# Graph network kernel, one core: the keys of the third pair of logits parted 330 and 330 instead of 512 and 148

## The chip, the cores and the metric

The kernel runs on one NeuronCore of one Trainium2 chip. The metric is device time in microseconds (us), start to end of one execution; a timed run is one such execution, and the number compared is the median of several. The names of the engines follow the profile: PE is TensorE (matmuls; PEld is its weight load), DVE is VectorE, ACT is ScalarE, POOL is GpSimd, SP is SyncE, which here only issues transfers.

## The reference

Two graph layers over N = 2708 nodes with D = 256 features, float32. Layer 0 adds one graph convolution to x and normalises. Layer 1 takes two steps. In each, an attention matrix over all nodes is made from queries and keys of width 64, thinned to the largest probabilities of each row that together hold 0.9, and multiplied on the features; beside it, the features are spread by the normalised adjacency matrix R. Cut to what matters:

```
q = X @ W1.T @ W2.T ;  k = X @ W3.T
logits = q @ k.T                       # 2708 x 2708, contraction over 64
probs  = softmax(logits)               # then the top-p entries of each row alone are kept
A      = kept / sum(kept)
R      = (S + I) / rowsum(S + I)
for n in 0, 1:
    A  = top_p_attention(Xa)
    Xf = R @ Xf
    Xa = A @ Xa
    Z  = Z + Xf @ U1[n].T + Xa @ U2[n].T
out = layernorm(X + Z), added to X and normalised again
```

## The kernel before, in words

Rows of the node set are worked on in 22 blocks of 128 (the last has 20). The features lie transposed in the on-chip memory where they feed projections, and block by block where they are multiplied by attention weights.

**Queries and keys.** `qk_project` (L420 on) makes queries and keys of a range of columns with one stationary operand of 128 columns, 64 of which give the key and 64 the query: two matmuls (L426) into one "misc" buffer of PSUM, and then three copies on ACT (L428, L429, L430): the query goes to both halves of the partitions, the key to one half only. Keys are kept in pairs of chunks: the first chunk of a pair lies on one half of the partitions, the second on the other, so that a pair of logits matmuls can use the two halves of the array. Chunks are 512 wide: 0, 512, 1024, 1536, 2048, 2560, and the last holds 148. In step 0 `qk_project` is called for one chunk at a time, in the loop over the adjacency matrix; in step 1 for one block of 128 columns, from `project` in `step1_out`, where it is followed by one more projection into a "misc" buffer (L699), whose sum with x is taken by DVE (L702). There are two "misc" buffers.

**Logits.** `logits(s, t, i)` makes pair i (0, 1, 2) of block t: two matmuls with a contraction of 64, one per half of the partitions, into the two banks of the one "lg" buffer (L507). Each float32 matmul is two records in the profile. ACT empties the buffer over both banks in one instruction: as a copy (L514) in the first attention step, as an exponential (L844, and L848 for the first pair) in the second. The third pair has 512 and 148 columns.

**Stages.** After the adjacency loop (28 to 286 us) comes a prologue: the logits of blocks 0, 1 and 2, three pairs each, with projections by U1 (L651) between them, then DVE's extraction of the largest candidates (L570, L577, L579), ACT's exponentials (L613) and DVE's mask (L635). Then the first attention step: 22 iterations of the block loop, 17.5 us each (343 to 718 us). In each, a block's weights are transposed on PE in six groups (L527), copied by ACT (L530) and multiplied on the features (L564); the logits of the block three ahead stand at groups 0, 1 and 2, and the projections of the block before (L692, L426, L699) at groups 2 and 3. POOL gathers the non-zero rows of the adjacency matrix meanwhile (L367). From 718 to 748 us the projections for the second step (L672) run, with the third pairs of the second step's blocks 0, 1 and 2 between them.

The second step (748 to the end) has a period of 23 to 24 us per block. PE transposes and multiplies the weights of one block (L527, L564), makes the logits of a later one (third pair at group 3 of six) and runs `r_units`, the products by R: 22 blocks for each of the two steps, of eight matmuls each (L749), the rows for which POOL gathers by indirect transfers, seven per block (L719), into two buffers. ACT and DVE search the threshold meanwhile (L966, L969 on ACT; L1023, L1030, L1039, L1083 and L1088 on DVE). POOL also does two elementwise instructions per finished block (L1207, L1208), for which ACT normalises first (L1192). The last gathered block of the first product by R has to be stored before the first gather of the second may start.

The order of the instructions on each engine is written out by hand: the lists and generators in the code fix it, and no scheduler changes it. PE and POOL, like the others, work in that order.

Of the kernel before, what the change touches and what calls it, by code (L numbers as in the profile page):

```python
# [9 lines left out]
FP = mybir.dt.float32  # L10
# [10 lines left out]
P = 128  # L21
CH = 512
# [20 lines left out]

def chunks(N):
    return [(a, min(N, a + CH)) for a in range(0, N, CH)]


class Common:
# [4 lines left out]
def gnn_two_layer_kernel(ctx: ExitStack, tc: tile.TileContext, N, xT_d, x_d, adj_d, w0_d, b0_d,  # L53
# [30 lines left out]
    assert SEG * (NS - 1) + 8 <= N <= SEG * NS == SEG2 * NS2 and N >= SEG2 * (NS2 - 1) + 8  # L84
    assert NB == 3 * KS + 1 and CW == P and CAP % 8 == 0 and N < NB * P
    CHS = chunks(N)
    KH = NB // 2

# [36 lines left out]
    with fast:  # L125
        fast_path(fast, tc, c, flags, fint, xT_d, x_d, w0_d, b0_d, w1_d, w2_d, w3_d, u1_d, u2_d, g_d, b_d)
# [22 lines left out]
def fast_path(ctx, tc, c, flags, fint, xT_d, x_d, w0_d, b0_d, w1_d, w2_d, w3_d, u1_d, u2_d, g_d, b_d):  # L149
    nc = tc.nc  # L150
    N, D, DA, NB, DC, KH, CHS, rows = c.N, c.D, c.DA, c.NB, c.DC, c.KH, c.CHS, c.rows
# [5 lines left out]
    big = ctx.enter_context(tc.tile_pool(name="big", bufs=1))  # L157
# [5 lines left out]
    def ps_lg():  # L163
        return ps.tile([P, 2, CH], FP, tag="lg", name="lg", bufs=1)
# [10 lines left out]
    def ps_misc():  # L175
        return ps.tile([P, CH], FP, tag="misc", name="misc")
# [91 lines left out]
    at = NB * (NB - 1)  # L268
# [119 lines left out]
    for t in range(NB):  # L388
        p = rows(t)
        py = ps_misc()  # L390
        for j in range(DC):
            nc.tensor.matmul(py[:p, :D], lhsT=xT[:, j, t * P:t * P + p], rhs=w0[:, DC + j, :],  # L392
                             start=j == 0, stop=j == DC - 1)
# [8 lines left out]


    q = big.tile([P, N], FP, tag="Q", name="q")
    keys = [big.tile([P, (len(CHS) + 1) // 2, CH], FP, tag=f"K{s}", name=f"k{s}") for s in range(2)]


    wqkq = small.tile([P, DC, 3, DA], FP, tag="wqkq", name="wqkq", bufs=1)
# [10 lines left out]
    def qk_project(s, a, b, src):  # L419


        n, i, h = b - a, a // CH // 2, a // CH % 2
        po = ps_misc()
        for j in range(DC):
            w = wqkq[:, j, 1 - h:3 - h].rearrange("p h a -> p (h a)")
            nc.tensor.matmul(po[:, :n], lhsT=w, rhs=src(j), start=j == 0, stop=j == DC - 1)  # L426
        own, other = (slice(DA * g, DA * g + DA) for g in (h, 1 - h))
        nc.scalar.copy(q[other, a:b], po[other, :n])  # L428
        nc.scalar.copy(q[own, a:b], po[other, :n])  # L429
        nc.scalar.copy(keys[s][own, i, a % CH:a % CH + n], po[own, :n])  # L430

    x1T = big.tile([P, DC, N], FP, tag="B", name="x1T")

# [7 lines left out]
    def x1_qk(i):  # L441
        a, b = CHS[i]
        qk_project(0, a, b, lambda j: x1T[:, j, a:b])
# [3 lines left out]
    for m in range(NB):  # L447
        p = rows(m)
# [12 lines left out]
        for j in range(DC):  # L461
            nc.tensor.matmul(acc[:p, :D], lhsT=xT[:, j, m * P:m * P + p], rhs=w0[:, j, :],  # L462
                             start=False, stop=j == DC - 1)
# [6 lines left out]
        h = work.tile([P, D], FP, tag="mid", name="h")  # L470
# [12 lines left out]
        if m >= ML:  # L483
            i = m - ML
# [9 lines left out]
    x1_transpose(NB - 1)  # L494
    x1_qk(len(CHS) - 1)

    NL = (len(CHS) + 1) // 2

    def logits(s, t, i):


        p = rows(t)
        lg = ps_lg()
        cs = CHS[2 * i:2 * i + 2]
        for h, (a, b) in enumerate(cs):
            o = slice(DA * h, DA * h + DA)
            nc.tensor.matmul(lg[:p, h, :b - a], lhsT=q[o, t * P:t * P + p], rhs=keys[s][o, i, :b - a],  # L507
                             start=True, stop=True)
        a, b = cs[0][0], cs[-1][1]
        return lg.rearrange("p h n -> p (h n)")[:p, :b - a], a, b  # L510

    def logits1(t, i):
        lg, a, b = logits(0, t, i)
        nc.scalar.copy(es[t % 4][:rows(t), a:b], lg)  # L514
# [165 lines left out]
    def step1_out(t, acc, ra):  # L680

        p = rows(t)
        xaT = xaT_all[:, :, t * P:t * P + p]
        xa = work.tile([P, D], FP, tag="in", name="xa", bufs=3)

        def scale():
            nc.scalar.activation(xa[:p], acc[:p, :D], AF.Copy, scale=ra[:p])

        def turn_out():
            tr = ps_tr()  # L690
            for j in range(DC):
                nc.tensor.transpose(tr[:, j, :p], xa[:p, j * P:(j + 1) * P], ident[:p, :p])  # L692
            nc.scalar.copy(xaT[:, :, :p], tr[:, :DC, :p])

        def project():
            qk_project(1, t * P, t * P + p, lambda j: xaT[:, j, :p])
            pz = ps_misc()
            for j in range(DC):
                nc.tensor.matmul(pz[:p, :D], lhsT=xaT[:, j, :p], rhs=c.u2[:, j, 0, :],  # L699
                                 start=j == 0, stop=j == DC - 1)  # L700
            za = work.tile([P, D], FP, tag="mid", name="za")
            nc.vector.tensor_add(za[:p], pz[:p, :D], x1[:p, t, :])  # L702
            nc.sync.dma_start(out=za_d[t * P:t * P + p, :], in_=za[:p])

        return scale, turn_out, project
# [144 lines left out]
    def begin_search(b):  # L850

        nc.vector.tensor_reduce(b.z, b.all[:b.p, :NL], AX.X, ALU.add)
        yield
# [13 lines left out]
    def begin1(t, n):  # L867
        nonlocal n_u
        for i in range(NL):
            logits1(t, i)  # L870
# [21 lines left out]
    at = {(m // 2, 3 * (m % 2) + 1): m for m in range(4)}  # L892
# [4 lines left out]
    for t in range(NB):  # L897
        acc = ps_acc(t)
        part = exps1(t + 2) if t + 2 < NB else None
        b = None  # L900
        if t >= NB - 3:
            b = blocks[t - (NB - 3)] = Block(t - (NB - 3))
        ra_next = finish1(t + 1) if t + 1 < NB else None
        for g in range(NG):
            turn(t, g, x1, acc, es[t % 4])
            if ends and 1 <= g <= 3:
                ends[g - 1]()
            if g < NL and t + 3 < NB:
                logits1(t + 3, g)
            if b and g in (0, 2):  # L910
                lg = logits(1, b.t, g // 2)
                if g == 0:
                    shift(b, lg[0])
# [33 lines left out]
    for t in range(3):  # L947
        exps2(blocks[t], 2, *logits(1, t, 2))
        ya_pair()
# [5 lines left out]
    w = tile1[:, NW:]  # L955
# [315 lines left out]
    lg = logits(1, 3, 0)  # L1271
# [3 lines left out]
    for per in range(NB + 2):  # L1275
# [11 lines left out]
        for g in range(NG):  # L1287
            n = n_r * (g + 1) // NG - n_r * g // NG
# [13 lines left out]
            if b_exp and g == 3:  # L1302
                lg = logits(1, b_exp.t, 2)
            if g == NG - 1 and 3 < per + 3 < NB:
                lg = logits(1, per + 3, 0)
            if g:
                r_units(n)
            if b_exp and g == 1:
                lg = logits(1, b_exp.t, 1)
# [8 lines left out]
            if g == 0:  # L1318
                final_slot(0)
                if t_mul:  # L1320
                    t = t_mul - 1
# [6 lines left out]
    t = EDGE  # L1328
# [24 lines left out]
    n = len(new) + len(finals)  # L1353
# [381 lines left out]
```

## Time and profile before

| | us |
|---|---|
| three timed runs, median | 1295.33 |
| their lowest and highest | 1294.3, 1296.72 |
| the profiled execution | 1291.2 |
| its span, first to last instruction | 1289.4 |

The page of the profile is of that one execution. Its first part gives, for each engine, the time in which it was busy, that as a share of the span, and the number of instructions. A group names line, engine, operation, what is written from what (out<-in), the shape, the count, busy time, mean ns of one, and the idle time of the engine just before, with what ended it. A wait names what the engine was released by. In the timeline, equal neighbours are merged into one row: start, length, and xcount. In the chain, each piece is followed back to what released it. The mean granted clock of PE was 0.986 of full speed. The 528 records of the logits matmuls (L507) had a median of 589 ns each.

### The profile page before, as it was taken

How to read it: one execution, taken by the hardware profiler on the slowest of the kernel's cores; microseconds unless marked ns; L12 is line 12 of the kernel's file. 1: busy time of each engine (PE TensorE's matmuls, PEld its weight loads, DVE VectorE, ACT ScalarE, POOL GpSimd, SP SyncE). 2: the span in 40 equal slices, each digit the busy share in tenths (PEclk: the TensorE clock that was granted, in tenths of full speed). 3: DMA queues.
4: the chain of work that ended last, by engine and by line, in shares of the span. 5: the costliest groups of instructions: out<-in, count | busy, mean ns of one | idle time of the engine just before them, and what ended most of it. 6: DMA issues, size and time to landing. Idle time of an engine off the chain costs nothing.

```text
span 1289.4 us, 18741 instructions
## 1 busy us (share of the span) xinstructions
PE 1226.3 (95%) x5764; PEld 888.1 (69%) x5764; DVE 973.9 (76%) x3252; ACT 735.5 (57%) x1337; POOL 635.9 (49%) x594
## 2 busy tenths in 40 slices
PE   8999999979899999999999987999999999999885
PEld 6878777843477777777777555777766777767664
DVE  2445545884999997977872179889888999999886
ACT  2000110125456656556655488887888989989822
POOL 1000000003475452577756058878874878888860
PEclk9999999999999999999999988999999999999998
DMA  7455445423322210122224244565563545565451
GB/s 196 152 193 170 143 149 168 149 90 107 121 82 83 72 57 28 43 88 91 93 85 100 63 149 150 178 189 177 180 154 118 179 155 154 165 195 158 145 139 39
DMA packets 101703, 165.99 MB, mean 129 GB/s; under 512 B 17362, under 2 KB 74070, under 8 KB 101594
## 3 DMA queue, kind: packets, MB, share of 16 engines
q1 hardware_dynamic: 75308, 108.65, 26.0%
q0 software_dynamic: 20544, 51.17, 14.3%
q10 hardware_dynamic: 5742, 4.89, 1.3%
q8 instruction: 48, 0.79, 0.2%
q14 instruction: 61, 0.50, 0.1%
HBM read 130.74 MB, written 33.90 MB: 128 GB/s over the span
## 4 chain that ended last, share of the span: by engine, by line
PE 79%; DVE 8%; ACT 7%; DMA 3%; POOL 2%; issue 2%; ACTq 0%; POOLq 0%; DVEq 0%
PE acc L564 27%; PE acc L257 16%; PE lg L507 9%; PE misc L749 8%; PE tr L527 7%; PE acc L651 2%; DMA yg<-v_d,ix 2%; PE acc L462 2%; PE misc L392 2%; PE misc L426 2%; PE acc L672 2%; ACT e L966 2%; PE misc L699 1%; DVE e L1088 1%; ACT e L844 1%
## 5 line engine op out<-in xcount | busy, mean ns | idle before, releaser
L530 ACT COPY wT<-tr 128x512 f32<-128x512 f32 (+2 forms) x258 | 132.1, 519 | 208.7 <-PE tr L527 208.7
L564 PE MATMUL acc<-x,wT 128*128 128x256 f32 (+1 forms) x924 | 230.5, 388 | 0.0
L564 PE MATMUL acc<-ya,wT 128*128 128x256 f32 (+1 forms) x924 | 227.1, 385 | 0.0
L719 POOL DMA_INDIRECT yg<-v_d,ix x154 | 194.8, 1265 | 59.6 <-issue 22.6
L564 PEld LDWEIGHTS acc<-x,wT 128*128 128x128 f32 (+1 forms) x924 | 165.2, 189 | 71.0 <-issue 37.4
L719 POOL DMA_INDIRECT yg<-yf_d,ix x154 | 188.2, 1222 | 48.3 <-issue 22.5
L257 PE MATMUL acc<-y,adj_t 128*128 128x257 f32 (+1 forms) x924 | 208.4, 381 | 0.0
L564 PEld LDWEIGHTS acc<-ya,wT 128*128 128x128 f32 (+1 forms) x924 | 170.2, 190 | 44.4 <-issue 24.0
L749 PE MATMUL misc<-yg,adj_t 128*128 128x256 f32 (+1 forms) x704 | 183.7, 394 | 14.9 <-DMA yg<-v_d,ix 5.9
L367 POOL DMA_INDIRECT adj_t<-in_adj,ix x154 | 171.3, 1112 | 52.0 <-issue 41.8
L257 PEld LDWEIGHTS acc<-y,adj_t 128*128 128x128 f32 (+1 forms) x924 | 171.8, 189 | 32.7 <-issue 8.9
L749 PEld LDWEIGHTS misc<-yg,adj_t 128*128 128x128 f32 (+1 forms) x704 | 123.6, 189 | 67.6 <-issue 23.4
L507 PE MATMUL lg<-k,q 64*128 64x512 f32 (+3 forms) x528 | 149.5, 594 | 13.7 <-ACT e L848 7.0
L527 PE MATMUL tr<-ident,e 128*128 128x128 f32 (+2 forms) x946 | 147.1, 274 | 3.1 <-DVE e L1088 2.0
L527 PEld LDWEIGHTS tr<-ident,e 128*128 128x128 f32 (+2 forms) x946 | 112.2, 138 | 44.8 <-issue 16.4
L334 POOL DMA_DIRECT2D part_d<-e x1 | 0.6, 573 | 285.6 <-DVE e L333 285.6
L439 ACT COPY x1T<-tr 128x256 f32<-128x256 f32 (+1 forms) x22 | 8.0, 364 | 186.6 <-PE tr L438 186.6
L966 ACT ACTIVATE e<-e,st 128x2708 f32<-128x2708 f32 (+1 forms) x43 | 113.5, 2639 | 0.1
L969 ACT ACTIVATE e<-e,st 128x2708 f32<-128x2708 f32 (+1 forms) x42 | 110.9, 2641 | 0.1
L570 DVE MAX8 cand<-e 128x8 f32<-128x170 f32 (+1 forms) x352 | 87.2, 318 | 26.7 <-ACT e L514 26.7
L1030 DVE MAX8 cand<-w 128x8 f32<-128x170 f32 (+1 forms) x352 | 94.2, 321 | 0.0
L1083 DVE MATCH_REPLACE8 w<-part,e 128x680 f32<-128x680 f32 (+1 forms) x88 | 74.3, 851 | 0.0
(238 smaller groups left out, 1696.4 us busy)
## 6 DMA issues: line engine op xcount, KB each, us to landing
adj_t<-in_adj SPq DMA_DIRECT2D x44, 704.0 KB
adj_t<-adjc_d SPq DMA_DIRECT2D x44, 448.0 KB
adjc_d<-adj_t SPq DMA_DIRECT2D x22, 256.0 KB
base<-za_d SPq DMA_DIRECT2D x40, 128.0 KB
adjc_d<-adj_t SPq DMA_DIRECT2D x22, 192.0 KB
xt<-in_x ACTq DMA_DIRECT2D x21, 128.0 KB
x_d<-x SPq DMA_DIRECT2D x21, 128.0 KB
x1b_d<-xb SPq DMA_DIRECT2D x21, 128.0 KB
```

The source lines that it names most:

```text
L257: nc.tensor.matmul(acc[:p, :n], lhsT=halves[k // KH][:kw, k % KH, :p], rhs=y[:kw, k, :n], start=k == 0, stop=stop and k == NB - 1)
L367: nc.gpsimd.indirect_dma_start(out=a[:CW, i, :], out_offset=None, in_=adj_rows, in_offset=bass.IndirectOffsetOnAxis(ap=ix[:CW, m, i:i + 1] ...
L507: nc.tensor.matmul(lg[:p, h, :b - a], lhsT=q[o, t * P:t * P + p], rhs=keys[s][o, i, :b - a], start=True, stop=True)
L527: nc.tensor.transpose(tr[:kw, k % 4, :p], e[:p, k * P:k * P + kw], ident[:p, :p])
L530: nc.scalar.copy(wT[:, :full, :p], tr[:, :full, :p])
L564: nc.tensor.matmul(acc[:p, :D], lhsT=wT[:kw, k % 4, :p], rhs=y[:kw, k, :], start=k == 0, stop=k == NB - 1)
L570: nc.vector.max(dst[:p, i * 8:(i + 1) * 8], src[:p, i * step:i * step + w])
L719: nc.gpsimd.indirect_dma_start(out=y[:CW, i, :], out_offset=None, in_=rows_d, in_offset=bass.IndirectOffsetOnAxis(ap=ix[:CW, m, i:i + 1], ...
L749: nc.tensor.matmul(acc[:p, :D], lhsT=a[:kw, k, :p], rhs=y[:kw, k, :], start=k == 0, stop=k == CC)
L966: nc.scalar.activation(scr[:b.p, :N], e, AF.Relu, bias=b.nz, scale=b.l[k], accum_out=b.relu)
L969: nc.scalar.activation(scr[:b.p, :N], e, AF.Sign, bias=b.nz, scale=b.l[k], accum_out=b.sign)
L1030: nc.vector.max(b.cand[:p, 8 * i:8 * i + 8], low[:p, SEG2 * i:SEG2 * (i + 1)])
```

## The change

The borders of the keys move. `key_parts` cuts N into ranges of 1024 columns and each range in the middle: 0, 512, 1024, 1536, 2048, 2378, 2708. The first four parts are as before; the third pair now has 330 and 330 columns. `logits` places the first half of a pair at the end of its bank (from column 182 of 512 for the third pair), so that the two halves still lie side by side across the border of the two banks, and ACT's instruction reads 660 columns as before. `qk_project` goes over the parts that a range of columns touches and does the whole of its work for each. In step 0 that divides the chunk of columns 2048 to 2560 in two (330 and 182); in step 1 it divides block 18, columns 2304 to 2432 (74 and 54). In the built program the first L699 matmul after block 18 waits for PE and ACT. Nothing else moves, and no transfer changes.

```diff
+def key_parts(N):
+    parts = []
+    for a in range(0, N, 2 * CH):
+        b = min(N, a + 2 * CH)
+        parts += [(a, (a + b) // 2), ((a + b) // 2, b)]
+    return parts
...
-    keys = [big.tile([P, (len(CHS) + 1) // 2, CH], FP, tag=f"K{s}", name=f"k{s}") for s in range(2)]
+    KPS = key_parts(N)
+    keys = [big.tile([P, len(KPS) // 2, CH], FP, tag=f"K{s}", name=f"k{s}") for s in range(2)]
...
-        n, i, h = b - a, a // CH // 2, a // CH % 2
-        po = ps_misc()
-        for j in range(DC):
-            w = wqkq[:, j, 1 - h:3 - h].rearrange("p h a -> p (h a)")
-            nc.tensor.matmul(po[:, :n], lhsT=w, rhs=src(j), start=j == 0, stop=j == DC - 1)
-        own, other = (slice(DA * g, DA * g + DA) for g in (h, 1 - h))
-        nc.scalar.copy(q[other, a:b], po[other, :n])
-        nc.scalar.copy(q[own, a:b], po[other, :n])
-        nc.scalar.copy(keys[s][own, i, a % CH:a % CH + n], po[own, :n])
+        for c_, (ka, kb) in enumerate(KPS):
+            lo, hi = max(a, ka), min(b, kb)
+            if lo >= hi:
+                continue
+            n, i, h = hi - lo, c_ // 2, c_ % 2
+            po = ps_misc()
+            for j in range(DC):
+                w = wqkq[:, j, 1 - h:3 - h].rearrange("p h a -> p (h a)")
+                nc.tensor.matmul(po[:, :n], lhsT=w, rhs=src(j)[:, lo - a:hi - a], start=j == 0, stop=j == DC - 1)
+            own, other = (slice(DA * g, DA * g + DA) for g in (h, 1 - h))
+            nc.scalar.copy(q[other, lo:hi], po[other, :n])
+            nc.scalar.copy(q[own, lo:hi], po[other, :n])
+            nc.scalar.copy(keys[s][own, i, lo - ka:hi - ka], po[own, :n])
...
-    NL = (len(CHS) + 1) // 2
+    NL = len(KPS) // 2
...
-        cs = CHS[2 * i:2 * i + 2]
+        cs = KPS[2 * i:2 * i + 2]
+        skip = CH - (cs[0][1] - cs[0][0])
         for h, (a, b) in enumerate(cs):
             o = slice(DA * h, DA * h + DA)
-            nc.tensor.matmul(lg[:p, h, :b - a], lhsT=q[o, t * P:t * P + p], rhs=keys[s][o, i, :b - a],
+            at = (skip, 0)[h]
+            nc.tensor.matmul(lg[:p, h, at:at + b - a], lhsT=q[o, t * P:t * P + p], rhs=keys[s][o, i, :b - a],
                              start=True, stop=True)
         a, b = cs[0][0], cs[-1][1]
-        return lg.rearrange("p h n -> p (h n)")[:p, :b - a], a, b
+        return lg.rearrange("p h n -> p (h n)")[:p, skip:skip + b - a], a, b
```

## The prediction

> **What bounds the kernel now.** I read the page's busy shares first, then busy time by stage, then the PE's timeline around the changed matmuls, then what POOL waits for, then the chain of work that ended last. The page:
>
> ```profile
> PE 1226.3 (95%) x5764; PEld 888.1 (69%) x5764; DVE 973.9 (76%) x3252; ACT 735.5 (57%) x1337; POOL 635.9 (49%) x594
> ```
>
> PE looks like the one bound, but 95% is a mean over stages. Busy time per stretch (start:end, length, then PE, PEld, DVE, ACT, POOL, clock, DMA share, GB/s), one block of step 1, then blocks of step 2:
>
> ```profile
> 413.60:431.10 17.50, 17.50 (x89) 12.71 (x88) 15.92 (x59) 10.54 (x21) 9.10 (x9) 1.00 0.22 69
> 854.43:878.21 23.78, 23.78 (x115) 17.98 (x115) 20.19 (x70) 19.92 (x33) 19.21 (x16) 1.00 0.60 190
> 1111.00:1134.48 23.48, 23.16 (x110) 16.87 (x110) 23.17 (x78) 22.13 (x39) 19.68 (x17) 1.00 0.57 174
> ```
>
> In step 1 PE has no gap and every other engine has 1.6 us to spare or more: PE alone sets the pace. In step 2 PE is still gapless, but look at POOL: 19.21 us in 16 instructions. What POOL waits for between 806 and 970 us (all its rows but three like them; total, times, longest):
>
> ```profile
> POOL yg L719 <- issue: 12.5, 41, 0.3
> POOL yg L719 <- PE misc L749: 9.5, 31, 0.3
> POOL yg L719 <- DMA yg<-yf_d,ix: 3.0, 10, 0.3
> ```
>
> No gap is longer than 0.3 us, whatever is named, and each gather has one: that is the cost of starting a gather, not a wait. 16 x 0.3 + 19.2 = 24.0 us against a period of 23.78: POOL is full too. It is so from its first gather of this stage at 750.2 to 965.0, and from 1047.6 to 1246.7 (no gap above 0.32 us in either stretch). Part of this is held by DVE, as the timeline shows:
>
> ```profile
> 823.72 3.05 DVE L1088 SCALAR_TENSOR_TENSOR e<-w,st,e 128x2720 f32<-128x2720 f32 x1
> 825.00 2.59 POOL L719 DMA_INDIRECT yg<-yf_d,ix  x1 [0.30 <-PE tr L527]
> 827.89 0.95 POOL L719 DMA_INDIRECT yg<-yf_d,ix  x1 [0.30 <-issue]
> ```
>
> A gather takes 0.95 us, but 2.59 when a long DVE instruction (L1088, L1023) runs: it ends 0.82 us after that one. Forty gathers of this stage do so. And the chain shows that PE has caught up with POOL by 955:
>
> ```profile
> 952.83 0.88 PE misc L749 x4
> 953.71 0.34 issue
> 954.05 0.94 POOL yg L719
> 954.99 0.30 issue
> 955.29 3.03 DMA yg<-yf_d,ix
> 958.37 0.70 PE misc L749 x2
> ```
>
> The matmuls that change, on PE's timeline of step 1 (start, length; a row is named after its first matmul):
>
> ```profile
> 349.70 1.12 PE L507 MATMUL lg<-k,q 64*128 64x512 f32 x4
> 350.75 1.99 PE L564 MATMUL acc<-x,wT 128*128 128x256 f32 x8
> ...
> 359.39 1.13 PE L507 MATMUL lg<-k,q 64*128 64x512 f32 x4
> 360.45 1.32 PE L564 MATMUL acc<-x,wT 128*128 128x256 f32 x4
> ```
>
> The first is a third pair (512 and 148 columns, two records each), the second a pair of 512 and 512. Both hold PE 1.05 to 1.06 us. The halves run at once, and the wider one sets the time.
>
> [...]
>
> **The change, part by part.** The sum is against the profiled execution (span 1289.4, time 1291.2); the three timed runs have a median 4.1 us above it, which I carry over unchanged.
>
> *A third pair.* Eight records of 256 columns (L564) take 1.73 us from start to start in the chain: 0.216 each, 0.845 ns a column. Each half needs two passes, so 512 to 330 removes 2 x 182 x 0.845 = 0.31 us; the pair of 148 let the next work start 0.007 earlier than a pair of 512 does, so I take 0.30. Bounds: 0, if halves of 330 did not overlap (330+330 is 512+148, so no loss), and 1.05 x 182/512 = 0.37, if the pair's fixed part shrank too. There are 44 of them, 22 blocks in 2 steps: 13.2 us of PE. How much arrives:
>
> - Prologue, 297.8, 311.9, 326.0: PE leads the chain until 316.7 (then ACT's exponentials and DVE's extraction). The first two count: 0.6.
> - Step-1 loop, 349.7 to 663.9: 19 pairs, no PE gap above 0.06 us. 19 x 0.30 = 5.7. DVE's 15.9 (16.7 in the busiest block) still fits in 17.2.
> - 734.0, 736.9, 739.9: the chain runs through these and the projections L672 to 748. 0.9. POOL's first gather (750.2) waits for PE's L749 at 749.2, so the whole gathering starts earlier by all up to here.
> - 771.7 to 936.6: 8 pairs. PE gains 2.4 us on POOL, but at 958.4 it already waits for POOL's gathers, which are full since 750. Counted 0.
> - 961.2: between that wait and the end of the last gathered block (972.4), which POOL awaits from 965.0 to 979.2. 0.3. The next, 983.0, lies in a stretch that the chain gives to ACT and DVE: 0.
> - 1005.1, 1028.1: PE leads; POOL stands 2.79 us before 1047.6 for ACT's L1192, and ACT's queue there starts from PE's transpose at 1040.6. 0.6.
> - 1051.0 to 1193.0: 7 pairs. From 1047.6 POOL is full, at 24.1 to 25.2 us for two gathered blocks against PE's 23; the chain ends in gathers from 1184.9. 0.
>
> *Block 18 in two pieces (74 and 54 columns).* Its projection in step 1, with what follows:
>
> ```profile
> 684.75 0.61 PE L426 MATMUL misc<-xaT_all,wqkq 128*128 128x128 f32 x4
> 685.20 1.03 PE L699 MATMUL misc<-u,xaT_all 128*128 128x256 f32 x4
> 685.56 0.26 ACT L428 COPY q<-misc 64x128 f32<-64x128 f32 x1
> ```
>
> Four records more at 0.11 us (four of 128 columns go from 684.75 to 685.20; narrower ones are taken no shorter): +0.45. And a new wait: there are two "misc" buffers, the pieces take both, so L699 now waits until ACT's three copies have emptied the first (about 0.22 each from 685.56: 686.2), where it would have started at 685.6: +0.65. Behind L699 stand the products L564 and all of PE; DVE's sum L702 waits for it, with 8 us to spare. Three more copies (+0.6) delay ACT's exponential at 686.27; nothing waits for it for 6 us. I take 1.2; ends 0.45 (no wait) and 1.8 (ACT late as well).
>
> *Columns 2048 to 2560 of step 0 in two pieces (at 270.5).* PE columns are the same. ACT's copies rise from 3 x 0.58 to about 3 x (0.43 + 0.31), +0.48, but may start 0.6 earlier, after the first piece; ACT's root L140 follows them on the chain. 0, ends -0.3 and +0.5. Reads of 660 logits still span two banks, same shape: 0.
>
> Sum: 0.6 + 5.7 - 1.2 + 0.9 + 0.3 + 0.6 = 6.9 us off. Span 1282.5, profiled 1284.3, median 1288.4.
>
> **Rivals.**
> 1. *All of PE's time arrives:* 13.2 - 1.2 = 12.0 us, 1283.3. For it: PE has no gap over most of 790 to 1133. Against: POOL's unbroken row of gathers.
> 2. *Step 1 gives less:* another engine holds step 1 once PE is shorter, or the wait at block 18 is repeated through ACT. With half of the loop's gain 4.0 us remain, 1291.3. Against: 1.6 us of spare time on DVE, 7 on ACT.
> 3. *Slower, by the gathers' phase:* some 40 gathers are held by DVE for 1.7 to 2.9 us, by where in the 1.25 us between gathers the long instruction begins. PE's shift moves DVE against POOL. If the mean hold grows by 6.9/40 = 0.17 us, the gain is gone; at +0.3 it is 12 - 6.9 = 5.1 us slower, 1300.4. For it: POOL is full for 400 us. Against: the phases look spread now, and a spread stays a spread.
> 4. *The halves do not overlap at 330:* no pair gains, 1.2 us lost: 1296.5. Against: pairs of 512 and 512 overlap.
>
> **How the numbers follow.** A measurement of this kernel can tell about 0.2%, 2.6 us. Forecast (5 to 9 us off) 0.62, its own range 1286.3 to 1290.3; rival 1 and what lies towards it 0.16; rival 2 0.12; rival 3 0.08, half of it within 0.2%; rival 4 0.02. From these: faster 0.88, same 0.07, slower 0.05. Range 1284.0 to 1292.0: it leaves out the far ends of rivals 1 and 2 and rivals 3 and 4.
>
> **What would show it.** Third pairs with 0.75 us from start to start in place of 1.05; step-1 blocks of 17.24 us; the first gather after the memset near 744; L699 after block 18 behind a wait of about 0.65 for ACT's copies; PE waiting more, some 2 us, for gathers before 965 and again after 1100, with POOL still gapless. If step-2 blocks before 950 shrink to 23.5 and no new wait for gathers shows, the argument on POOL is wrong and rival 1 holds. If gathers' mean length moves from 1.24 us, rival 3 is at work.

## The result, and the profile after

The changed kernel takes 1288.06 us (median of five runs, 1286.94 to 1290.43) against 1295.33 (median of five, 1294.3 to 1296.72) for the kernel before on the same chip: ratio 0.9947, 95% interval 0.9934 to 0.9959, which is 7.3 us less, with 5.3 and 8.5 as the ends. (The ratio is of the means of the runs; the two medians alone give 0.9944. Where a ratio below differs from that of the medians beside it, the ratio is the figure with the interval.) The prediction on record was 1288.4.

The profiled execution of the changed kernel took 1286.94 us, span 1285.1, mean granted clock of PE 0.981. Against the profile of before that is only 4.3 us less, and the sum on record had this profile at 1284.3; experiment 5 shows why one pair of profiles is a poor measure of the total. Lines have moved: the logits are L522 (before: L507), the transposes L542 (L527), ACT's copies of them L545 (L530), the attention products L579 (L564), the projections of queries and keys L439 and their copies L441 to L443 (L426, L428 to L430), the product that follows L714 (L699), the gathers L734 (L719), the products by R L764 (L749), ACT's exponentials L859 and L863 (L844, L848).

Busy time, its share of the span and the instructions, from the page of after:

```profile
PE 1219.4 (95%) x5772; PEld 894.0 (70%) x5772; DVE 973.0 (76%) x3252; ACT 736.1 (57%) x1343; POOL 626.1 (49%) x594
```

PE has 8 records more and is busy for 6.9 us less, though 13 us of matmul time were cut and half a microsecond added. Most of the rest is likely half speed: apart from the last 14 us, PE ran at half its clock for 37.5 us here and for 27.3 in the profile of before, which stretches its work by up to 5. A total hides where that went; the stages don't. Busy time by stretch (start:end, length, then PE, PEld, DVE, ACT, POOL, clock, DMA share, GB/s), the same three kinds of stretch as were shown of before:

```profile
410.53:427.77 17.24, 17.24 (x89) 12.72 (x88) 15.96 (x59) 10.57 (x20) 9.13 (x9) 1.00 0.23 70
851.70:875.18 23.48, 23.48 (x117) 17.96 (x115) 20.15 (x70) 19.92 (x33) 18.90 (x15) 1.00 0.60 188
1107.10:1130.50 23.40, 22.81 (x111) 16.80 (x110) 23.09 (x77) 22.01 (x40) 19.67 (x17) 1.00 0.55 174
```

A block of step 1 takes 17.24 us, where it took 17.54 (359.39 to 376.93 in before), and PE still has no gap in it. A block of step 2 before 950 us is shorter too (23.48, where the one shown of before took 23.78), so PE gained there at first. In the last row PE has 22.81 us of work in 23.40: the gain has turned into waiting.

The matmuls themselves, PE's timeline in step 1 (start, length of the merged row):

```profile
349.40 0.83 PE L522 MATMUL lg<-k,q 64*128 64x330 f32 x4
350.16 1.99 PE L579 MATMUL acc<-x,wT 128*128 128x256 f32 x8
...
358.80 1.13 PE L522 MATMUL lg<-k,q 64*128 64x512 f32 x4
```

A third pair now holds PE for 0.76 us from its start to the next, not 1.05. All 44 of them did so, 0.296 us less each; the pairs of 512 and 512 stay at 1.06.

Block 18, in two pieces (timeline, PE and ACT; the bracket is the idle time before the row and what ended it):

```profile
678.83 1.00 PE L439 MATMUL misc<-xaT_all,wqkq 128*128 128x74 f32 x8
...
679.64 0.22 ACT L441 COPY q<-misc 64x74 f32<-64x74 f32 x1
...
680.09 0.21 ACT L443 COPY k<-misc 64x74 f32<-64x74 f32 x1
...
680.36 1.13 PE L714 MATMUL misc<-u,xaT_all 128*128 128x256 f32 x4 [0.54 <-ACT k L443]
```

Eight records in place of four, and the wait that was forecast: L714 stands until ACT's third copy has emptied the first of the two misc buffers.

What POOL waited for from 803 to 967 us (total, times, longest), the two largest of six rows:

```profile
POOL yg L734 <- issue: 14.6, 48, 0.3
POOL yg L734 <- PE misc L764: 9.8, 32, 0.3
```

As before, no gap in any row is longer than the 0.3 us that each gather has, so POOL is full. The same holds for its second unbroken row, over the gathers of the second product (1046 to 1245 us; the two largest of six rows):

```profile
POOL yg L734 <- issue: 15.7, 52, 0.3
POOL yg L734 <- PE misc L764: 7.9, 26, 0.3
```

PE runs into the first of the two rows in the chain of work that ended last (start, length, what):

```profile
945.71 0.45 PE misc L764 x2
946.15 0.07 issue
946.23 5.00 DMA yg<-yf_d,ix
951.23 0.04 issue
951.27 0.70 PE misc L764 x2
```

### The profile page after: what moved, and what is told of

Its sections match the earlier page's. It is cut to its first block, busy times and chain, and to the rows that moved or that the text cites. A ratio compares the mean times of both kernels' runs of the same rounds, so it can differ in the third digit from the quotient of the medians.

```text
span 1285.1 us, 18764 instructions
## 1 busy us (share of the span) xinstructions
PE 1219.4 (95%) x5772; PEld 894.0 (70%) x5772; DVE 973.0 (76%) x3252; ACT 736.1 (57%) x1343; POOL 626.1 (49%) x594
## 4 chain that ended last, share of the span: by engine, by line
PE 79%; DVE 8%; ACT 8%; DMA 3%; issue 2%; POOL 1%; ACTq 0%; POOLq 0%; DVEq 0%
PE acc L579 27%; PE acc L265 16%; PE lg L522 8%; PE misc L764 8%; PE tr L542 7%; PE acc L666 2%; DMA yg<-v_d,ix 2%; PE acc L475 2%; PE misc L400 2%; ACT e L981 2%; PE acc L687 2%; PE misc L714 2%; PE misc L439 2%; DVE e L1103 1%; ACT e L984 1%
## 5 line engine op out<-in xcount | busy, mean ns | idle before, releaser
L545 ACT COPY wT<-tr 128x512 f32<-128x512 f32 (+2 forms) x258 | 131.9, 518 | 210.5 <-PE tr L542 208.8
L579 PE MATMUL acc<-x,wT 128*128 128x256 f32 (+1 forms) x924 | 230.5, 388 | 0.0
L579 PE MATMUL acc<-ya,wT 128*128 128x256 f32 (+1 forms) x924 | 228.1, 386 | 0.0
L734 POOL DMA_INDIRECT yg<-v_d,ix x154 | 190.5, 1237 | 59.3 <-issue 22.7
L734 POOL DMA_INDIRECT yg<-yf_d,ix x154 | 187.5, 1217 | 48.3 <-issue 24.3
L579 PEld LDWEIGHTS acc<-x,wT 128*128 128x128 f32 (+1 forms) x924 | 165.3, 190 | 65.3 <-issue 31.7
L579 PEld LDWEIGHTS acc<-ya,wT 128*128 128x128 f32 (+1 forms) x924 | 171.2, 191 | 44.2 <-issue 23.7
L764 PE MATMUL misc<-yg,adj_t 128*128 128x256 f32 (+1 forms) x704 | 184.9, 396 | 15.5 <-DMA yg<-v_d,ix 7.4
L375 POOL DMA_INDIRECT adj_t<-in_adj,ix x154 | 165.3, 1074 | 51.8 <-issue 39.2
L764 PEld LDWEIGHTS misc<-yg,adj_t 128*128 128x128 f32 (+1 forms) x704 | 124.3, 190 | 63.1 <-issue 25.2
L522 PE MATMUL lg<-k,q 64*128 64x512 f32 (+3 forms) x528 | 138.0, 600 | 14.4 <-ACT e L863 7.0
L542 PE MATMUL tr<-ident,e 128*128 128x128 f32 (+2 forms) x946 | 147.8, 275 | 3.6 <-ACT wT L545 2.7
L542 PEld LDWEIGHTS tr<-ident,e 128*128 128x128 f32 (+2 forms) x946 | 113.0, 139 | 45.8 <-issue 15.5
```

The costliest lines, as they stand in the source:

```text
L375: nc.gpsimd.indirect_dma_start(out=a[:CW, i, :], out_offset=None, in_=adj_rows, in_offset=bass.IndirectOffsetOnAxis(ap=ix[:CW, m, i:i + 1] ...
L522: nc.tensor.matmul(lg[:p, h, at:at + b - a], lhsT=q[o, t * P:t * P + p], rhs=keys[s][o, i, :b - a], start=True, stop=True)
L542: nc.tensor.transpose(tr[:kw, k % 4, :p], e[:p, k * P:k * P + kw], ident[:p, :p])
L545: nc.scalar.copy(wT[:, :full, :p], tr[:, :full, :p])
L579: nc.tensor.matmul(acc[:p, :D], lhsT=wT[:kw, k % 4, :p], rhs=y[:kw, k, :], start=k == 0, stop=k == NB - 1)
L734: nc.gpsimd.indirect_dma_start(out=y[:CW, i, :], out_offset=None, in_=rows_d, in_offset=bass.IndirectOffsetOnAxis(ap=ix[:CW, m, i:i + 1], ...
```

## The experiments

The lead of the changed kernel is used below: at one and the same pair of logits, the start in the kernel before less the start in the changed kernel, each from its own span's beginning. It says where time was gained and lost, and a constant difference at the start of the execution drops out between two rows. Times on the left are those of the first profile of before; "relieved" is experiment 2.

| lead in us at | first profiles | profiles a | profiles b | relieved |
|---|---|---|---|---|
| 350, after the prologue | 0.29 | 1.39 | 3.10 | 0.72 |
| 675, before block 18 | 5.93 | 7.03 | 8.74 | 6.36 |
| 692, after block 18 | 4.74 | 5.84 | 7.54 | 5.17 |
| 734, the first third pair of step 2 | 1.95 | 4.35 | 7.68 | 3.84 |
| 748, just before the first gather | 2.85 | 5.24 | 8.57 | 4.73 |
| 970, past the first product's gathers | 3.20 | 5.18 | 8.53 | 6.66 |
| 1058 | 4.03 | 6.07 | 9.41 | 7.55 |
| 1152 | 4.08 | 6.11 | 9.40 | 7.58 |
| difference of the spans | 4.3 | 7.0 | 9.2 | 7.5 |

**Experiment 1: one step at a time.** The theory puts nearly all of the gain in step 1; the first rival has every third pair pay, in both steps. The new borders were given to one step's keys alone (for the second step with the two lists exchanged), beside both kernels. On the chip that these four ran on the kernel before took 1344.16 us, so its times are not set beside those of the others, only ratios taken on it.

```diff
-    KPS = key_parts(N)
+    KPS = [key_parts(N), CHS]
...
-        for c_, (ka, kb) in enumerate(KPS):
+        for c_, (ka, kb) in enumerate(KPS[s]):
...
-        cs = KPS[2 * i:2 * i + 2]
+        cs = KPS[s][2 * i:2 * i + 2]
```

First step alone:

> Keys parted 330 and 330 for the first attention step only; the second step keeps 512 and 148, so block 18's projection stays whole. Theory (PE sets the pace of the first step, POOL's gathers that of the second): two pairs of the prologue and 19 of the loop count, 21 x 0.30 = 6.2 us off, as much as the whole change or a little less (0.6 to 0.9 us short of it plus the 1.2 us of block 18 saved). Rival (every pair's PE time arrives, wherever it stands): 22 x 0.30 = 6.5 us off, and the second step alone must then give the other half. Rival (the loss of PE's clock seen at 710 us in the profile after comes from the first step's change): the clock falls to half there again.

Second step alone:

> Keys parted 330 and 330 for the second attention step only; the first keeps 512 and 148. Block 18 is projected in two pieces. Theory: 22 pairs remove 6.6 us of PE time, but only three before 748 us (0.9), one at 961 (0.3) and two or three after 1005 (0.6 to 0.9) count, less 1.2 for block 18: 0.6 to 0.9 us off at most, within what can be told from nothing; PE's waits for gathers grow by some 2 us before 960 and again after 1050. Rival (every pair's PE time arrives): 6.6 - 1.2 = 5.4 us off.

The changed kernel, and the kernel before once more:

> The changed kernel again, for its run to run spread and for PE's half-speed stretches. Theory: 7 us off again; whether the half-speed stretch of 6.8 us near 710 us, which cost 2.8 us in its first profile, is there, differs between executions. Rival: the change brings it about, and it is there in every profile of the changed kernel.

> The kernel before again, against itself, for its spread and for PE's half-speed stretches. Theory: ratio 1; its first profile (1291.2 us, 4.1 us under its timed median) had one half-speed stretch fewer than others do, so another profile shows one near 715 us and a time nearer 1295. Rival: the kernel before has no such stretch, and its profile was short for another reason.

| new borders in | ratio to the kernel before | 95% interval |
|---|---|---|
| first step | 0.9939 | 0.9913 to 0.9964 |
| second step | 0.9991 | 0.9974 to 1.0009 |
| both (the changed kernel) | 0.9928 | 0.9904 to 0.9951 |
| neither | 1.0004 | 0.9980 to 1.0029 |

The second step's 22 pairs are 6.5 us of PE time, less 1.2 for block 18. Had they arrived, its ratio would be 0.9960, and that is outside the interval. The first step alone gives the gain of the whole within the intervals. The first rival falls; which cover swallows the second step's pairs is not told by this. The chip is also not like the others in one stretch of step 2: in all four profiles the 140 gathers of the first product took 230 to 232 us, with a longest gap of 2.5 to 2.9 us, where experiment 2 has 213 to 216 and no such gap. So POOL was not full in that stretch on this chip, and what covers the pairs in it may be something else there.

**Experiment 2: POOL relieved.** Every seventh gather of a block becomes a plain load on SP's queue, in both kernels. It was meant to tell POOL's unbroken row of gathers from PE alone as the bound of step 2.

```diff
-        for i in range(CC):
+        nc.sync.dma_start(out=y[:CW, CC - 1, :], in_=(c.yf_d, c.v_d)[s][:CW, m, :])
+        for i in range(CC - 1):
```

> The kernel before, but of the seven gathers of a block that POOL issues in step 2 the seventh is replaced by a plain load of the block's own 128 rows on SP's queue, so those rows are other rows than the reference's. The amount of data and the matmuls stay. It takes 2 of 16 POOL instructions (2 x 1.54 us, gather and gap) from each 24 us of step 2: POOL needs about 21, PE 23.8. Theory (POOL's gathers bound PE late in each half of step 2): PE no longer waits for gathers, and the end, which is a chain of gathers from 1184 us on, comes earlier: 3 to 8 us faster than the kernel before (0.994 to 0.998). Rival (PE alone bounds step 2): within 2 us of the kernel before (0.9985 to 1.0015), POOL only gets gaps.

> The changed kernel with the same replacement of every seventh gather by a plain load. Theory (POOL full, so the 15 third pairs of 771 to 937 and of 1051 to 1193 us give nothing in the changed kernel): with POOL relieved they arrive, 15 x 0.296 = 4.4 us more, so that this kernel against the relieved kernel before is 10 to 12 us faster (ratio of their ratios 0.9910 to 0.9925) where the changed kernel against the kernel before was 7.3; in the traces, the lead of the changed kernel's third pairs grows by 0.296 at each pair from 770 to 940 and from 1050 to 1190 us, away from stretches of lower clock. Rival (PE alone): the lead is the same 7 us with and without the relief, 0.9945.

On a chip where the kernel before took 1295.07 us, the relieved kernel before took 1284.54 (0.9910, 0.9884 to 0.9936). That is more than the 3 to 8 us expected, and the rival of 2 us at most falls; of the 7.1 us between the two profiled spans 4.8 come after the last pair of logits (1193 us), where the chain of before runs through gathers. The relieved changed kernel took 1275.92 (0.9842, 0.9824 to 0.9860). Between the two lie 8.6 us, ratio 0.9842/0.9910 = 0.9931. That is neither the 10 to 12 us of the theory nor the 7.3 of the rival, and too close to the latter for the intervals to part them. The traces do part them, and the answer is different in the two stretches.

*770 to 970 us.* In the table the lead grows by 1.93 us from 748 to 970 when POOL is relieved: eight steps of 0.296, from the pair at 793 on, less 0.43 lost between 748 and 790, where half speed falls on other work in the two kernels (the pair at 772 lies in there). Without the relief it grows by 0.35, -0.06 and -0.04. What POOL waits for in the relieved changed kernel (its lines from the gathers on are one further down), 803 to 950 us, has gaps up to 2.6 us in its largest row:

```profile
POOL yg L735 <- PE misc L765: 21.8, 30, 2.6
```

and from 787 to 960 PE waits for no gather. In all eight profiles with full gathers that were taken on chips of this pace (experiments 2 to 5 and the first two), the 140 gathers of this stretch take 213.2 to 215.9 us from the first start to the last end, with no gap above 0.32. So here POOL is the cover, as forecast: the lead of PE grows and is handed back at waits for gathers. In profiles b it went from 8.57 us at 748 to 9.77 at 848 and was 8.53 at 970. PE's wait for gathers from 787 to 975 us, kernel before, then changed kernel, both of profiles b:

```profile
PE misc L749 <- DMA yg<-yf_d,ix: 0.4, 1, 0.4
```

```profile
PE misc L764 <- DMA yg<-yf_d,ix: 2.9, 4, 1.3
```

In profiles a the same row grew from 0.6 to 3.2 us, in the first profiles, where half speed had already taken 1.24 us of the lead at 779 to 788, from 0.2 to 0.7 only.

*1060 to 1190 us.* Here the lead stays at 7.55 to 7.59 us with POOL relieved: six third pairs and no gain at all. The expectation had POOL as the only cover, and that is not enough. The period of both relieved kernels is 23.19 us (1091.63 to 1114.82 before, 1084.07 to 1107.26 changed), and the changed one has a wait that the other lacks. The relieved changed kernel's timeline:

```profile
1093.69 0.57 ACT L545 COPY wT<-tr 128x512 f32<-128x512 f32 x1
...
1094.31 0.33 PE L542 MATMUL tr<-ident,e 128*128 128x128 f32 x1 [0.26 <-ACT wT L545]
...
1103.90 0.59 ACT L545 COPY wT<-tr 128x512 f32<-128x512 f32 x1 [0.64 <-PE tr L542]
```

It is a ring of two engines. Once in each period ACT waits for PE's transposes (the last row, 0.64 us), and once PE's transposes wait for ACT's copy (the middle row). From the one wait to the other ACT waits for nobody, from about 1080.7 (1103.90 less the period) to 1094.26; then PE has no gap, from 1094.31 to the transposes that ACT awaits at 1103.90. The third pair (1090.43) lies in ACT's part of the ring, where PE isn't on the path. The kernel before was already in it: there the eight matmuls ahead of the same transposes take 1.86 us from start to start (1099.12 to 1100.98) where 1.73 is usual: 0.13 more, and PE's waits from 1066 to 1178 us have no row for ACT. In the relieved changed kernel they take 2.15 (1092.16 to 1094.31): 0.13 and the 0.30 taken off the pair.

The ring is there with full gathers too. PE's waits in the changed kernel itself, 1062 to 1174 us, largest row:

```profile
PE tr L542 <- ACT wT L545: 1.3, 5, 0.3
```

These are five waits of 0.27 us, one behind each third pair of that stretch; the kernel before has no such row. With the border of experiment 4 the same waits are 0.19: a pair that is shortened by 0.08 less is followed by a wait that is 0.08 shorter. On the chip of experiment 1 the lead stays flat as well, within 0.04 us from 1117 to 1210 (times of its kernel before), for the second step alone and for the whole change. No run took work off ACT, so the ring is read from traces and not tried.

With full gathers POOL holds all the same. Its row of the second product takes 201.0 to 202.1 us in all eight profiles, with no gap above 0.31, so nothing that PE gains after its start brings its end forward. It starts 3.8, 5.8 and 9.1 us earlier in the changed kernel (first, a, b), which is the lead at 1044 us (3.7, 5.8, 9.1), and the spans differ by 4.3, 7.0 and 9.2. So the traces show two covers in the kernel as it is; that the ring is enough alone is shown by relieving POOL, that POOL would be is not tried.

**Experiment 3: one misc buffer for block 18.** The two pieces share one buffer, and the copies of the later piece come first, so that the other buffer is free for the product.

```diff
+        pieces = []
+        whole = ps_misc() if s else None
...
-            po = ps_misc()
+            po = whole[:, lo - a:hi - a] if s else ps_misc()
...
+            pieces.append((lo, hi, ka, n, i, h, po))
+        for lo, hi, ka, n, i, h, po in pieces[::-1]:
```

> The changed kernel, but the two pieces of block 18's projection in step 1 share one misc buffer, the copies of the later piece first; the other of the two buffers is then free for the next product. Theory (0.65 of the 1.18 us that block 18 lost was the new wait for ACT's copies): no wait ahead of that product beyond 0.1 us; from the pair before block 18's projection to the one after it the kernel loses 0.5 to 0.6 us against the kernel before, not 1.18; total 0.6 us under the changed kernel, which timed runs can't tell. Rival (the loss is the four more records and their weight loads): the loss stays near 1.2 us.

Its timeline at block 18 (the product is L718 here):

```profile
679.76 0.99 PE L441 MATMUL misc<-xaT_all,wqkq 128*128 128x74 f32 x8
...
680.59 1.09 PE L718 MATMUL misc<-u,xaT_all 128*128 128x256 f32 x4
```

The product starts 0.83 us after the pieces, with no wait. From 675 to 692 us this kernel loses 0.45 us against the kernel before, the changed kernel 1.19: the wait costs 0.74, the four more records 0.45. In total it takes 1288.38 us (0.9945, 0.9927 to 0.9963), which can't be told from the changed kernel. What is gained at 680 us doesn't show at the end by more than the scatter.

**Experiment 4: another border.** The third pair is parted at the edge of block 18, 384 and 276 columns.

```diff
-        parts += [(a, (a + b) // 2), ((a + b) // 2, b)]
+        mid = (a + b + P) // 2 // P * P
+        parts += [(a, mid), (mid, b)]
```

> The changed kernel with the border of the third pair at column 2432, the edge of block 18, so that the pair has 384 and 276 columns and no block is projected in two pieces in step 1 (columns 2048 to 2560 of step 0 still are). Theory (two passes of the wider half at 0.845 ns a column, and 1.18 us for the split block): third pairs of 1.053 - 2 x 128 x 0.845 ns = 0.837 us, each 0.216 us shorter than before; no loss at block 18; lead over the kernel before at 675 us 20 x 0.216 = 4.3 us and the same 4.3 after block 18, against 5.9 and 4.7 with 330; total near 5.5 to 6 us off (0.9955), within 1.5 us of the changed kernel. Rival (the time of a pair follows something other than the wider half, such as the sum or the count of columns rounded to 512): the third pairs stay at 1.05 or fall to 0.757.

PE's timeline in step 1:

```profile
350.35 0.91 PE L523 MATMUL lg<-k,q 64*128 64x384 f32 x4
351.19 1.99 PE L580 MATMUL acc<-x,wT 128*128 128x256 f32 x8
```

A pair holds PE for 0.84 us, and the lead grows by 0.213 a block: the wider half alone sets the time, 213 ns for 2 x 128 columns fewer, 0.83 ns a column. From 675 to 692 us nothing is lost. The total is 1291.03 us (1286.13 to 1291.89; 0.9949, 0.9927 to 0.9971): no better than the border in the middle. From 350 to 692 us it gains 4.05 us of lead, the changed kernel 4.45. The expected 5.5 to 6 us in total can be neither confirmed nor denied: the medians give 4.0 off, the ratio 6.6.

**Experiment 5: the clock.** In the first profiles the lead fell from 4.74 us at 716 to 1.95 at 734, and no part of the change lies between. Both kernels wait 1.98 us there for ACT's exponential, and the changed one then ran PE at half speed. Busy time by stretch of the changed kernel (the number after the engines is the granted clock):

```profile
706.87:710.29 3.42, 2.21 (x21) 1.35 (x20) 0.00 (x0) 2.37 (x6) 0.00 (x0) 1.00 0.00 0
710.29:713.70 3.41, 2.64 (x12) 0.67 (x12) 0.00 (x0) 1.10 (x4) 0.00 (x0) 0.50 0.00 0
```

To see whether that belongs to the change or to the execution, both kernels were profiled twice more as they are, with no edit, on a further chip; these are the profiles a and b. The four profiles of experiment 1, whose expectations ask the same question, are counted too.

> The kernel before, unchanged, profiled once more. In the first pair of profiles the changed kernel ran PE at half speed from 710.3 to 717.1 us, after PE's 2 us of waiting for ACT's exponentials, and lost 2.8 us of its lead there; the kernel before waited as long at 714 to 716 and kept full speed. Theory (the stretches of half speed lie on a grid of 3.41 us that stands anew in each execution, so the loss belongs to the execution and not to the change): in some of these four profiles the kernel before has such a stretch of 3.4 or 6.8 us at 714 to 721, at a cost of 1.4 to 2.8 us, and then takes 1292.5 to 1295 us, or the changed kernel lacks it. Rival (the change puts the wait where half speed always follows): the kernel before has none or at most one of 3.4 us, the changed kernel 6.8 us each time.

> The kernel before, unchanged, profiled a further time. The same two theories: by the first it has a stretch of half speed at 714 to 721 us in some executions and not in others, by where its grid of 3.41 us stands; by the rival none, or at most one of 3.4 us.

> The changed kernel, unchanged, profiled once more. By the first theory the stretch of half speed after the wait at 709 to 711 us varies between executions (0, 3.4 or 6.8 us), and without it the kernel takes about 2.8 us less than 1286.9; by the rival it is 6.8 us again.

> The changed kernel, unchanged, profiled a further time: by the first theory 0, 3.4 or 6.8 us of half speed after the wait at 709 to 711 us, by the rival 6.8 us again. In each of the four the third pairs before 690 us keep their distance of 0.296 us a block between the two kernels, whatever the clock does later.

| half speed after this wait, us | |
|---|---|
| kernel before: first, a, b; relieved; in experiment 1 | 0, 0, 3.4; 3.4; 10.2 |
| changed kernel: first, a, b; relieved; in experiment 1 | 6.8, 3.4, 3.4; 6.8; 0 |
| other edits of the changed kernel: one buffer, other border | 6.8, 6.8 |
| new borders in the first step alone, in the second alone | 6.8, 3.4 |

The two stretches below are of the kernel before, profile b, with the same kind of loss: 3.4 us at half speed after a stretch in which PE was busy for 1.42 of 3.40 us.

```profile
716.70:720.10 3.40, 1.42 (x13) 0.44 (x12) 0.00 (x0) 2.33 (x7) 0.00 (x0) 1.00 0.00 0
720.10:723.50 3.40, 3.40 (x20) 2.52 (x12) 0.00 (x0) 1.33 (x5) 0.00 (x0) 0.50 0.03 5
```

And these two are of the changed kernel in experiment 1, around the end of the same wait (740.02 us there), at full clock:

```profile
738.44:741.85 3.41, 1.82 (x15) 0.65 (x16) 0.00 (x0) 1.89 (x7) 0.00 (x0) 1.00 0.00 0
741.85:745.27 3.42, 3.42 (x38) 2.09 (x40) 0.43 (x1) 2.32 (x7) 0.00 (x0) 1.00 0.12 40
```

The rival falls: the loss differs between executions of one kernel, the changed kernel was free of it once, and the kernel before had it in three of five, up to 10.2 us. By the two profiles of single steps it isn't tied to the first step's borders either. Whether the change makes it likelier stays open: the changed kernel was free of it in one of five, the kernel before in two of five, and the chip of experiment 1 ran PE at half speed for 65 to 82 us in all, where the others did for 27 to 41. It costs 1.5 us where it lasts 3.4 and 2.8 where it lasts 6.8. Between 779 and 788 us, in another stretch of half speed that both kernels have, the first profiles lose a further 1.24 us of lead, a lose 0.38, and b gain 0.32. The expectation for the time of a profile with such a stretch was off: profile b of before took 1296.38 us, and the one without, a, 1295.25. They differ from the first (1291.2) mostly by their start: the first logits come at 287.80 and 289.41 us in a and b, at 286.76 in the first, and at 293 the distance is 1.7 and 2.9 us. The first profile of before was an early one, which is why the first pair of profiles shows 4.3 us where the runs show 7.3. Profiles a and b differ by 7.0 and 9.2 us in time.

## Why the prediction was right

Its sum, term by term; "measured" is the growth of the lead over the same stretch in the first profiles, a and b, taken before rounding:

| step | predicted us | measured us |
|---|---|---|
| prologue, two pairs | 0.6 | 0.59 in each |
| step-1 loop, 19 pairs | 5.7 | 5.64, 5.64, 5.64 |
| block 18 | -1.2 | -1.19, -1.19, -1.20 |
| the clock, 716 to 734 | not in the sum | -2.78, -1.48, +0.15 |
| three pairs before the first gather | 0.9 | 0.89 in each |
| eight pairs, 772 to 937, and the one at 961 | 0 and 0.3 | together 0.35, -0.06, -0.04 |
| 983; 1005 and 1028 | 0; 0.6 | with the pair at 1051: 0.84, 0.89, 0.88 |
| seven pairs from 1051 on | 0 | 0.3 for the first (counted above), 0.04, 0.04, -0.01 for the others up to 1152 |
| sum | 6.9 | 6.9 with the means of the rows, less the clock's; with it 4.4, 5.3, 6.9 |

**The size of a pair.** Two passes of the wider half, 0.30 us, measured 0.296; the other border gave 0.213 where 0.216 was worked out in the same way. The fourth rival, halves that do not overlap, falls.

**Block 18.** The two parts were forecast as 0.45 for the records and 0.65 for the wait; experiment 3 measured 0.45 and 0.74. The added copies on ACT had 6 us of cover, as forecast: the lead doesn't change between 692 and 716 us.

**POOL's cover up to 965.** Right, and shown by relieving POOL. (The 24.0 us that the prediction gave POOL in a block of 23.78 count 16 instructions; 15 start in it, 19.17 us and 15 gaps of 0.30, which is 23.7. The reading stays: full.) One sign named in advance would have misled alone: blocks of step 2 did shrink to 23.5, and in the first profiles PE waited only 0.5 us more for gathers; profiles a and b have the forecast 2 us and more (2.6, 2.5). After 1100 us the waits ahead of the products by R grew by 3.2 us in b only (0.1 and -0.8 in the others). The pair at 961 was counted at 0.3 and gave that in one of three comparisons, where the growth can as well come from gathers held a little less. The first gather was forecast near 744 and came at 747.4, 746.7 and 746.1, between 2.8 and 8.6 us earlier than in before. The gain claimed up to there was 6.0; the lead grew by 3.1, 4.4 and 6.1 us, and the clock row is what it missed.

**The seven pairs after 1051: right in size, one cover of two seen.** The step gave them 0 because POOL is full from 1047.6, and it is: with full gathers its row runs on unbroken to the end of the gathers. But with POOL relieved the pairs gave nothing either, except the first, which gave 0.3 and stands outside the ring, so POOL is not all that covers them: the ring of ACT's queue and PE's transposes takes them too. The view of waits has no row for it in the kernel before, where it shows only as 0.13 us more from start to start; ACT's 22.3 us of work in a period of 23.2 did show that something like it was near, and the prediction passed over that.

**What was left out.** The granted clock. A term of 1.5 to 2.8 us, as large as block 18, came and went after a wait that was there before, and the sum had no room for it. That the median came within 0.4 us of the forecast is luck at this scale: two terms were off and cancelled. The sum put the profiled execution at 1284.3 us, and it took 1286.9; the 4.1 us from profile to median were carried over from the kernel before, and here they were 1.1. What the terms bear out is a gain near 7 us. If the clock struck both kernels in some executions, it falls out of the difference of the medians; that was not measured over the timed runs.

**The third rival: the gathers' phase.** It took some forty gathers of step 2 to be held by DVE, and forty it was in the first profile of before (18 of 140 from 750 to 965 us, 22 in the second product). Why DVE holds a gather no run here shows; the traces show that held gathers take 2.6 to 3.8 us and end 0.81 to 0.83 us after the DVE instruction (L1023 or L1088), where the others take 0.94 to 0.99. That a spread stays a spread held: the 140 gathers took between 213.2 and 215.9 us in eight profiles, never the 7 us more that would have taken the gain. What phase there is shows as a wait here and there: the kernel with the other border waited 2.3 us for gathers between 787 and 966 us.

**Columns 2048 to 2560 in two pieces.** Not settled. The bounds were -0.3 and +0.5 us, and the first logits start between 286.8 and 289.4 us from one execution to the next, with the old columns or the new.

The first rival (12 us) falls by experiment 1, and on the other chips by the lead, which grows by 0.8 to 1.2 us from 748 to 1152. The second (4 us, from a step 1 bound elsewhere or a block 18 repeated) falls by 5.64 us in the loop and a single loss of 1.19.

## What to carry to other kernels

A pair of row tiles cost what its wider half costs at all three splits tried here (1.05 us at 512 and 148 columns, 0.84 at 384 and 276, 0.76 at 330 and 330), so an uneven split is time that can be had, but only where PE is on the path: count the instances stage by stage, and give those behind another full engine nothing. An engine at 96% of a period beside one at 100% can be a second bound and not spare time, as ACT was here (22.3 us of work in 23.2); ask which wait would end last once the first bound is shorter, and look for start-to-start times that are a tenth of a microsecond too long, since the 0.13 us here stood in no row of the waits. To find a few microseconds, compare positions of the same instruction in two traces, not totals, and take more than one profile of each kernel.

## What the runs showed of the hardware that was not expected

- PE's half speed comes in steps of 3.41 us on a grid: within one execution all its stretches begin at the same remainder by 3.41333 us (0.64 for all seven of before, 0.31 for all nine of the changed kernel, whose first and last begin 996.69 us apart, 292 steps), and between executions the remainder differs (0.89, 1.58, 2.50, 3.27 in profiles a and b). It followed steps in which PE was busy for 2.21 of 3.42 us (710 us in the changed kernel) and for 1.42 of 3.40 (720 us in before, b), and even 2.88 of 3.41 (741 us in before, experiment 1), while 1.59 of 3.42 (714 us, first profile of before) and 1.82 of 3.41 (738 us in the changed kernel, experiment 1) were not followed by it. PE's busy time in the step before does not decide it in these five cases; what does stays open.
- Records of 74 and 54 columns cost about as much as records of 128 at the same weights: eight of them take 0.83 us in experiment 3, 0.10 each, where four of 128 columns take 0.45 in the kernel before, 0.11 each.
- A gather's price on POOL did not move with any edit: on chips of this pace 140 of them took 213.2 to 215.9 us, gaps included, with full gathers. Taking two of each 16 POOL instructions away (with other rows loaded in their place) made the kernel before 0.9% faster, more than the change that this document is about.
